# Small bf16 products ahead of unmasked scores, and products of zeros in TensorE's first waits

## The chip, the cores and the metric

The kernel runs on one core of a Trainium2 chip. The metric is the device time of one execution in microseconds, given as the median of several runs. The engines are called PE (TensorE; PEld is its weight load), DVE (VectorE), ACT (ScalarE), POOL (GpSimd) and SP (SyncE, which issues the DMAs).

## The reference

Eight batches of 512 tokens with 256 channels pass through two layers. Each layer is attention, added to its input, and a feed-forward part, added to that. Cut to what matters here (`D` is 16, there are 16 heads):

```
# layer 0, attention on y = layernorm(x): two softmaxes, one causal over the tokens, one over the context
att  = where(causal, (y Wq + bq)(y Wk + bk)^T / sqrt(D), -inf)     # "S": masked scores
attc = (y Wcq + bcq)(ctx Wck + bck)^T / sqrt(D)                    # "C": no mask
x = x + (softmax(att) (y Wv + bv) + softmax(attc) (ctx Wcv + bcv)) Wp + bp
x = x + bitlinear(gelu(bitlinear(layernorm(x))))                   # quantised feed-forward
# layer 1
x = x + (softmax((y Wq + bq)(ctx Wk + bk)^T / sqrt(D)) (ctx Wv + bv)) Wo + bo   # "X": no mask, y = layernorm(x)
x = x + qlinear(gelu(qlinear(layernorm(x))))                       # quantised over the whole tensor
```

## The kernel before

**Units.** The attention work is cut into 24 units: `S`, `C` and `X` for each batch (`UNITS`). A unit has four groups of four heads, 96 groups in all (`G`). Two groups share a "stack": queries and keys are split into a high and a low part and laid by DMA into 48 rows of `qk_t` for each half of the partitions (rows 0 and 64), so that one product gives the scores of one head with more precision than one part holds. `stack_job` issues six DMAs of 256 KB for it.

**Three kinds of steps** pass over each group:

- `max_one` computes scores with queries on the partitions into a pair of PSUM banks (two heads at once, one in each half of the rows), and DVE reduces each row to its maximum. For `C` and `X` a step is one tile of 128 queries by 512 keys; for `S` the causal mask comes first.
- `rows_job` turns the maxima and lays them into rows 48 and 49 of the stack, so that the next scores come out with the maximum taken off.
- `exp_one` computes the scores again, keys on the partitions, 50 rows deep, into two banks, and ACT takes the exponential of each.
- `av_part` multiplies the exponentials with the values, four heads side by side in tiles of 128 rows by 32 columns.

For `S` units `masks` puts the mask into the bank before the scores: for each half of the rows two small bf16 products of an identity and a mask (64 rows), and the scores accumulate onto them. `C` and `X` units have no such products; there the first score product begins the bank.

**Tile shapes.** The projections, the values and the output products go through `wide`, four column tiles of 128x32 side by side ("cols"). Scores and masks use two row tiles of 64x128 ("rows"). Other products use the whole array ("full"). A "visit" in this text is a stretch of row-tiled steps between two stretches of the other kinds.

**The order** is not written by hand. The class `Plan` holds a clock for each engine and costs for each step, and a loop at the end of `build` takes, at each moment, the step or job that is due: maxima, exponentials, values, or one of the jobs (projections, feed-forward, evacuations), which are generators that yield the time when they want to go on. `plan.pe(cols, mode)` adds a step's cost and notes the tile shape in `plan.mode`; a change of shape costs `SWITCH`. The order that comes out is fixed at build time, and each engine works through its own list. `Writer.matmul` adds, for the first product into a bank under a new name, waits for all who read the bank before.

**The start.** `first_x` and the first two weights are loaded by DMA, then eight small DMAs of biases and eight of identity and mask are issued by SP. `ln_job` for the first tokens takes statistics in `stats` (four `bn_stats`, four `bn_aggr`), DVE normalises, PE turns the tokens (32 products, two records each in the profile), and `prep_job` for the first two stacks projects queries and keys; DVE and ACT split them, `stack_job` stacks them by DMA, and only then can the first scores run.

Of the kernel before, what the change touches and what calls it, by code (L numbers as in the profile page):

```python
# [9 lines left out]
BF16 = mybir.dt.bfloat16  # L10
SYNC = mybir.DependencyInfo(mybir.DependencyClass.Sync, mybir.DependencyReason.DATA)
# [5 lines left out]
NB, T, C, CC, H, D, FF = 8, 512, 256, 128, 16, 16, 1024  # L17
P = 128
# [206 lines left out]
GQ, AHEAD = 4, 3  # L225
LINGER = 0.2
ROW_COLS = 600
DVE_HANDICAP = 0.8


# [56 lines left out]
def build(tc, A, out):  # L287
    nc = Engines(tc)
# [8 lines left out]
    plan = Plan()  # L297
# [6 lines left out]
    pairs, banks = nc.pairs, nc.banks  # L304
# [44 lines left out]
    zero = const.tile([P, 1], F32, name="zero")  # L349
    nc.vector.memset(zero, 0.0)  # L350
    one = const.tile([P, 1], F32, name="one")
    nc.vector.memset(one, 1.0)
    ones_sq = one.broadcast_to([P, P])

    ident2 = const.tile([P, 2, P], BF16, name="ident2")
    mask2 = const.tile([P, 2, P], BF16, name="mask2")
# [105 lines left out]
    def used(key, tag, t):  # L462

        uses[key][0] -= 1
        uses[key][1] = max(uses[key][1], t)
        if not uses[key][0]:
            give(tag, uses[key][1])

    def stats(x, nm):

        st = wp.tile([P, NT, 6], F32, tag="bnst", name=f"st_{nm}", bufs=3)
        mv = wp.tile([P, NT, 2], F32, tag="bnmv", name=f"mv_{nm}", bufs=3)
        r = wp.tile([P, NT], F32, tag="rstd", name=f"r_{nm}", bufs=3)
        neg = wp.tile([P, NT], F32, tag="nmean", name=f"nm_{nm}", bufs=3)
        for t in range(NT):
            nc.vector.bn_stats(st[:, t, :], x[:, t, :])
            op("dve", C)
            yield plan.now + 0.4
        for t in range(NT):
            nc.vector.bn_aggr(mv[:, t, :], st[:, t, :])  # L480
        te = plan.run("dve", 0.4)
        nc.gpsimd.tensor_scalar(r, mv[:, :, 1], LN_EPS, 0.0, ALU.add, ALU.add)
        nc.gpsimd.tensor_tensor(r, r, mhalf, ALU.pow)
        nc.gpsimd.tensor_scalar(neg, mv[:, :, 0], -1.0, 0.0, ALU.mult, ALU.add)
        te = plan.run("pool", 1.3, te)
        return mv[:, :, 1], neg, r, te
# [63 lines left out]
    def prep_job(n):  # L550
        kind, b = UNITS[n // 2]
        u = n % 2
        yield from take("qkt")
        tt = tile("qkt", [P, 4, T], F32R, f"qkt{n}")
        tl = []

        def split(wname, ps, pb, tm, hi, lo):

            full = tt[:, lo, :].bitcast(F32)
            nc.scalar.activation(full, ps, AF.Identity, bias=qk_bias[:, BIDX[wname], u : u + 1])  # L560
            t = op("act", T + 110, tm)
            give_bank(pb, t)
            yield t + LAT
            if n < 2:
                nc.vector.tensor_copy(tt[:, hi, :], full)
                th = op("dve2", T, t)
                nc.vector.tensor_tensor(tt[:, lo, :], full, tt[:, hi, :].bitcast(F32), ALU.subtract)
                tl.append(op("dve", T))
            else:
                copy_ts(tt[:, hi, :], full)  # L570
                th = op("pool", T, t)
                low_part(tt[:, lo, :], full, tt[:, hi, :])
                tl.append(op("pool2", T, th))
            return th

        ready = []
        for i, (hi, lo) in enumerate(((0, 1), (3, 2))):
            wname, which = KIND[kind][i]
            key, ring = src_key(kind, b, which)
            yield from until(key, ("w", wname, u))  # L580
            xs = xlt[key]
            nk = xs.shape[1]
            ps, pb = yield from gen_bank()
            for k in range(nk):
                yield pe_next()
                wide(ps, WT[wname][:, u, k], xs[:, k, :], k == 0, k == nk - 1)
                tm = plan.pe(4 * T, "cols")
            used(key, ring, tm)
            ready.append((wname, ps, pb, tm, hi, lo))
            if n >= 2 or i == 1:  # L590
                for r in ready:
                    th = yield from split(*r)
                ready = []
        qkt_t[n] = (tt.bitcast(F32), tl)
        at["qkt", n] = max(tl[0], th)
# [50 lines left out]
    def masks(ps, c, blocks, keys):  # L646
# [5 lines left out]
        for k in range(2):  # L652
# [5 lines left out]
                start=k == 0, stop=False, skip_group_check=True,  # L658
            )

    def max_ready(s):
        G, i = MAX_STEPS[s]
        t = plan.bank_at("sm")
        if ("stack", G) not in at or t is None or (i == 0 and G % 2 == 0 and not plan.rings["mx"]):
            return None
        return max(at["stack", G], t)

    def max_one(s):

        G, i = MAX_STEPS[s]  # L670
        kind, _ = UNITS[G // 4]
        p, qts = MAXS[kind][i]
        n = G // 2
        if i == 0 and G % 2 == 0:
            heapq.heappop(plan.rings["mx"])
            mx_t[n] = tile("mx", [P, 2, 4, NT], F32, f"mx{n}")
        pb = plan.bank_take("sm")
        ps = pairs[pb // 2]
        pair = 2 * (G % 2) + p
        size = [(qt + 1) * P if kind == "S" else T for qt in qts]  # L680
        offs = [sum(size[:x]) for x in range(len(qts))]
        if kind == "S":

            first = size[0] // P - 1
            step = size[-1] // P
            for c in range(2):
                masks(ps[:, c], c, slice(first, first + (len(qts) - 1) * step + 1, step), False)
            plan.pe(len(qts) * 192 + 60, mode="rows")
        for off, w, qt in zip(offs, size, qts):
            for c in range(2):  # L690
                q, k = (qk_t[n % NQK][64 * c : 64 * c + 48, pair, x] for x in range(2))
                nc.tensor.matmul(
                    ps[:, c, off : off + w], q[:, qt * P : (qt + 1) * P], k[:, :w],
                    start=off == 0 and kind != "S", stop=True, skip_group_check=True,
                )
        t = plan.pe(sum(size), mode="rows")
        for off, w, qt in zip(offs, size, qts):
            nc.vector.tensor_reduce(
                mx_t[n][:, :, pair, qt], ps[:, :, off : off + w], AX.X, ALU.max, negate=True
            )  # L700
            t = op("dve", 2 * w, t)
        plan.bank_give("sm", pb, t)
        if s + 1 == len(MAX_STEPS) or MAX_STEPS[s + 1][0] != G:
            at["max", G] = t
# [51 lines left out]
    def exp_one(s):  # L756


        G, i = EXP_STEPS[s]
        kind, _ = UNITS[G // 4]  # L760
        p, kts = EXPS[kind][i]
        n = G // 2
        pair = 2 * (G % 2) + p
        pb = plan.bank_take("st", 2)
        tp, slots = zip(*(heapq.heappop(plan.p_free) for _ in range(2)))
        pt = [wp.tile([P, T], F32, tag=f"p{slots[c]}", name=f"p{G}_{i}_{c}", bufs=1) for c in range(2)]
        ps, off = [banks[x] for x in pb], 0
        if kind == "S":
            step = (T - kts[0] * P) // P
            for c in range(2):  # L770
                masks(ps[c], c, slice(0, (len(kts) - 1) * step + 1, step), True)
            plan.pe(len(kts) * P + 80, mode="rows")
        for kt in kts:
            q0 = kt * P if kind == "S" else 0
            w = T - q0
            for c in range(2):
                q, k = (qk_t[n % NQK][64 * c : 64 * c + 50, pair, x] for x in range(2))
                nc.tensor.matmul(
                    ps[c][:, off : off + w], k[:, kt * P : (kt + 1) * P], q[:, q0:],
                    start=off == 0 and kind != "S", stop=True, skip_group_check=True,  # L780
                )
                p_t[G, kt, 2 * p + c] = pt[c][:, off : off + w]
            off += w
        t = plan.pe(off, mode="rows")
        if s + 1 == len(EXP_STEPS) or EXP_STEPS[s + 1][0] != G:
            at["exp", G] = t
        tm = t
        for c in range(2):
            nc.scalar.activation(pt[c][:, :off], ps[c][:, :off], AF.Exp, scale=0.25)
            t = op("act", off, tm, tp[c])  # L790
            plan.bank_give("st", pb[c], t, c == 1)
        for kt in kts:
            p_at[G, kt, p] = t
        p_slots[G, kts[-1], p] = slots
# [799 lines left out]
    for bs in ((0,), (1,), (2, 3), (4, 5), (6, 7)):  # L1594
        n, b = len(bs), bs[0]
        if b == 4:
            split_b2()
        for f in range(8):
            i = 8 * b + n * f
            ps = [banks[2 + i % 6]] if n == 1 else [pairs[1 + f % 3][:, x] for x in range(2)]  # L1600
# [86 lines left out]
    for i in range(2 * NB):  # L1687
# [4 lines left out]
        ps = half_ps.pop(i, None)  # L1692
        if ps is None:
            ps = bias_first(i)
# [79 lines left out]
```

## Time and profile before

| | us |
|---|---|
| median of 3 runs | 1464.75 |
| lowest and highest | 1461.56 to 1465.69 |
| the profiled execution's own time | 1460.25 |
| its span, first to last instruction | 1458.4 |
| mean granted TensorE clock over the span | 0.971 |

| engine | busy us | share | instructions |
|---|---|---|---|
| PE | 1374.8 | 94% | 14400 |
| PEld | 597.5 | 41% | 14400 |
| DVE | 1142.0 | 78% | 1591 |
| ACT | 1035.5 | 71% | 1904 |
| POOL | 681.6 | 47% | 1025 |

All engines work at once, so the shares are not to be added. Products on PE overlap in the records: a product's record runs from its start to its end, and the next one may start before that end, so the distance from one start to the next tells more than the length of a record. A float32 product has two records, a product of the stacks (marked f32 in the profile) or of bf16 has one. `48*128` in a row of the profile means 48 rows and 128 columns of the array. The granted clock is the share of TensorE's full clock that the chip let through in a window of time.

### The profile page before, as it was taken

The numbers are of one execution on the slowest core, as the hardware profiler recorded it, in microseconds if no ns is written. First come the engines' busy times: TensorE is split into PE (matmuls) and PEld (weight loads), VectorE is DVE, ScalarE is ACT, GpSimd is POOL, SyncE is SP. The second block draws the span as 40 slices with busy tenths as digits, with TensorE's granted clock in tenths as the row PEclk, the third lists the DMA queues.
The fourth block names the chain that finished last, engine by engine and source line by source line (L and its number), as shares of the span: only waits on it lengthen the run. The fifth ranks groups of instructions, "written<-read, shape, count | busy, mean of one in ns | idle before, by whom it ended". The sixth has DMA issues, their size and how long they took to land. (4 is left out here: it accounts for less than half of the span.)

```text
span 1458.4 us, 36089 instructions
## 1 busy us (share of the span) xinstructions
PE 1374.8 (94%) x14400; PEld 597.5 (41%) x14400; DVE 1142.0 (78%) x1591; ACT 1035.5 (71%) x1904; POOL 681.6 (47%) x1025
## 2 busy tenths in 40 slices
PE   4999999999999999999999999999999998999978
PEld 2443444444444444434344433443333333333527
DVE  4678588697788886898777996689899888766397
ACT  1456767677768867767677777668778795777587
POOL 1463355465455465464653552654455541524332
PEclk8899999999999999999899999999999999999899
DMA  6593565667576755665457655556647657373343
GB/s 126 152 216 76 133 139 125 142 138 182 132 161 150 161 129 141 156 161 126 105 126 155 163 126 132 142 120 160 163 105 169 155 149 196 105 176 110 117 142 116
DMA packets 155612, 207.03 MB, mean 142 GB/s; under 512 B 71940, under 2 KB 74244, under 8 KB 154932
## 3 DMA queue, kind: packets, MB, share of 16 engines
q1 hardware_dynamic: 155444, 204.73, 58.0%
q8 instruction: 113, 1.85, 0.5%
q14 instruction: 55, 0.45, 0.1%
HBM read 68.15 MB, written 47.43 MB: 79 GB/s over the span
## 5 line engine op out<-in xcount | busy, mean ns | idle before, releaser
L241 DVE TENSOR_REDUCE mx<-pair 128x2 f32<-128x1024 f32 (+3 forms) x768 | 808.9, 1086 | 210.7 <-PE pair L259 194.6
L241 ACT ACTIVATE p<-bank 128x512 f32<-128x512 f32 (+1 forms) x1408 | 712.0, 587 | 232.7 <-PE bank L259 224.8
L259 PE MATMUL bank<-p,v 128*32 128x512 f32 (+3 forms) x3072 | 371.7, 563 | 2.9 <-DVE mrow L241 1.3
L259 PE MATMUL bank<-qk 50*128 50x512 f32 (+3 forms) x1536 | 337.6, 433 | 16.2 <-ACT p L241 8.0
L259 PE MATMUL pair<-qk 48*128 48x512 f32 (+3 forms) x1536 | 325.5, 438 | 25.7 <-DVE mx L241 11.8
L259 PEld LDWEIGHTS bank<-qk 50*128 50x128 f32 x1536 | 159.6, 190 | 215.7 <-ACT p L241 142.9
L259 PEld LDWEIGHTS pair<-qk 48*128 48x128 f32 x1536 | 148.0, 191 | 171.5 <-DVE mx L241 83.4
L384 POOL TENSOR_SCALAR qkt<-qkt 128x512 fp32r<-128x512 f32 x92 | 57.1, 621 | 164.1 <-ACT qkt L241 157.5
L241 ACT ACTIVATE qkt<-bank,qk_bias 128x512 f32<-128x512 f32 x96 | 66.6, 693 | 81.0 <-PE bank L259 65.4
L409 POOL TENSOR_TENSOR qkt<-qkt 128x512 fp32r<-128x512 f32 x92 | 118.8, 1291 | 7.7
L259 PEld LDWEIGHTS bank<-p,v 128*32 128x32 f32 x3072 | 70.9, 109 | 114.6 <-issue 85.9
L384 POOL TENSOR_SCALAR mhl<-mx 128x32 fp32r<-128x32 f32 x48 | 11.8, 245 | 171.3 <-DVE mx L241 164.8
L883 POOL TENSOR_TENSOR yt<-oc,rb 128x512 f32<-128x512 f32 x31 | 39.8, 1283 | 73.3 <-DMA rb<-scrz 50.9
L259 PE MATMUL pair<-mask,ident 64*128 64x128 bf16 (+2 forms) x768 | 58.0, 226 | 6.9 <-DVE mx L241 4.7
L259 PE MATMUL bank<-ident,mask 64*128 64x64 bf16 (+1 forms) x768 | 52.7, 206 | 3.7 <-ACT p L241 1.2
L259 PEld LDWEIGHTS <-ident 64*128 64x128 bf16 x768 | 26.1, 97 | 71.0 <-issue 52.8
L259 PEld LDWEIGHTS <-mask 64*128 64x128 bf16 x768 | 25.8, 96 | 69.3 <-issue 61.0
L241 ACT COPY v<-bank 128x512 f32<-128x512 f32 x44 | 26.2, 596 | 39.4 <-PE bank L259 39.1
L241 ACT COPY ev<-bank 128x512 f32<-128x512 f32 x56 | 33.5, 598 | 17.9 <-PE bank L259 17.9
L241 DVE SCALAR_TENSOR_TENSOR h<-bank,so,bc_l_b 128x512 f32<-128x512 f32 x64 | 45.3, 741 | 0.9 <-PE bank L259 0.7
L241 ACT ACT_TABLE_LOAD x34 | 43.6, 1283 | 1.9 <-PEq L1762 0.7
L1189 POOL TENSOR_SCALAR h<-h,sh 128x1024 f32<-128x1024 f32 x32 | 36.0, 1125 | 17.7 <-DVE sh L241 15.2
(230 smaller groups left out, 1686.4 us busy)
## 6 DMA issues: line engine op xcount, KB each, us to landing
qk<-qkt SPq DMA_DIRECT2D x288, 256.0 KB
scro<-ev SPq DMA_DIRECT2D x94, 256.0 KB
oc<-scro SPq DMA_DIRECT2D x47, 256.0 KB
rb<-scrz SPq DMA_DIRECT2D x47, 256.0 KB
x_d<-xb SPq DMA_DIRECT2D x15, 512.0 KB
xa_s<-in_x SPq DMA_DIRECT2D x8, 512.0 KB
xb<-in_x SPq DMA_DIRECT2D x8, 512.0 KB
xr<-x_d SPq DMA_DIRECT2D x16, 256.0 KB
```

The lines of the kernel that those rows point to most:

```text
L241: r = f(*args, **kw)
L259: r = self.eng.matmul(out, *args, **kw)
L384: nc.gpsimd.tensor_scalar(dst, src, 1.0, 0.0, ALU.mult, ALU.add)
L409: nc.gpsimd.tensor_tensor(dst, full, high.bitcast(F32), ALU.subtract)
L883: nc.gpsimd.tensor_tensor(y, o, rb, ALU.mult)
L1189: nc.gpsimd.tensor_scalar(ht, ht, s[:, t - t0 : t - t0 + 1], MAGIC, ALU.mult, ALU.add)
```

## The change

Two things are added; nothing is taken away, and `Plan` is not told of either, so its order of steps stays as it is.

1. `first_of_visit` is called at the head of every unmasked step of `max_one` and `exp_one` when `plan.mode` is not `rows`, that is when the step follows column-tiled or whole-array products. It issues, for each half of the rows, one bf16 product of 64 rows by 128 columns over 16 moving columns (`NFIRST`), of the identity and the mask, into the first 16 columns of the bank that the scores are about to begin. The scores start the bank anew, so nothing of it stays.
2. `keep_warm` issues products of zeros: a zero column spread to 128x128 as weights, and spread to 512 moving columns, into bank 6 (through `pairs[3]`). There are eight right after the constants are set, two behind each of the four `bn_stats` of the first tokens and three more behind the last of them, and 24 after the last projection of the second stack.

```
+NFIRST = 16
...
+    zero_b = zero.bitcast(BF16)[:, 0:1]
+
+    def keep_warm(n, behind=None):
+
+        for _ in range(n):
+            r = nc.tensor.matmul(
+                pairs[3][:, 0], zero_b.broadcast_to([P, P]), zero_b.broadcast_to([P, T]), start=True, stop=True
+            )
+            if behind is not None:
+                tc.add_manual_dep(r.ins, behind.ins.name, SYNC, reason="warm")
+                behind = None
+
+    keep_warm(8)
...
-            nc.vector.bn_stats(st[:, t, :], x[:, t, :])
+            r_st = nc.vector.bn_stats(st[:, t, :], x[:, t, :])
+            if nm == "s0":
+                keep_warm(2, r_st)
...
         te = plan.run("dve", 0.4)
+        if nm == "s0":
+            keep_warm(3, r_st)
...
             used(key, ring, tm)
+            if (n, i) == (1, 1):
+                keep_warm(24)
...
+    def first_of_visit(ps):
+
+
+        if plan.mode != "rows":
+            for c in range(2):
+                rows = slice(64 * c, 64 * c + 64)
+                nc.tensor.matmul(
+                    ps[c][:, :NFIRST], ident2[rows, 0], mask2[rows, 0, :NFIRST], start=True, stop=True,
+                    skip_group_check=True,
+                )
...
             plan.pe(len(qts) * 192 + 60, mode="rows")
+        else:
+            first_of_visit([ps[:, c] for c in range(2)])
...
             plan.pe(len(kts) * P + 80, mode="rows")
+        else:
+            first_of_visit(ps)
```

## The prediction

> **What bounds the kernel now.** I read the page's engine shares first, then busy time by stage, then TensorE's waits, then the order of time around single visits to the scores, then the start.
>
> ```profile
> PE 1374.8 (94%) x14400; PEld 597.5 (41%) x14400; DVE 1142.0 (78%) x1591; ACT 1035.5 (71%) x1904; POOL 681.6 (47%) x1025
> PEclk8899999999999999999899999999999999999899
> ```
>
> TensorE (PE) leads; its granted clock is low only in the first slices. By stage (us, then busy time and count of PE, its weight loads PEld, DVE, ACT, POOL; then clock, DMA share, GB/s):
>
> ```profile
> 400.00:800.00 400.00, 386.70 (x4494) 168.59 (x4487) 323.63 (x469) 290.38 (x542) 206.41 (x304) 0.97 0.63 143
> 800.00:1200.00 400.00, 385.19 (x3970) 154.56 (x3966) 338.56 (x456) 306.56 (x579) 201.76 (x308) 0.99 0.60 143
> ```
>
> From 64 to 1365 us, where the attention steps run, PE is idle for 46 of 1301 us, in 94 gaps over 0.1 us; VectorE and ScalarE have a fifth free. TensorE's largest waits there (us in total, times, longest):
>
> ```profile
> PE pair L259 <- DVE mx L241: 13.4, 25, 1.6
> PE bank L259 <- ACT p L241: 9.8, 18, 2.2
> ```
>
> So time added to TensorE in the middle mostly reaches the end, and a gain there mostly too, until one of these two becomes late. Now one unmasked visit, column-tiled products (128*32), then three score steps of 512 columns (start, duration):
>
> ```profile
> 661.34 1.06 PE L259 MATMUL bank<-p,v 128*32 128x512 f32 x8
> 662.34 0.50 PE L259 MATMUL pair<-qk 48*128 48x512 f32 x2
> 662.68 0.40 PE L259 MATMUL bank<-qk 50*128 50x512 f32 x2
> 662.91 0.40 PE L259 MATMUL pair<-qk 48*128 48x512 f32 x2
> ```
>
> The first step holds TensorE from 662.34 to 662.68, the second only to 662.91. The medians over the trace are 338 ns for a first step and 237 for a following one: a visit pays 101 ns at its door. That is the weight load: it starts 2 ns before the first product[...]. A visit that has masks ahead, products first and then the loads:
>
> ```profile
> 805.14 0.23 PE L259 MATMUL bank<-ident,mask 64*128 64x64 bf16 x4
> 805.21 0.48 PE L259 MATMUL bank<-qk 50*128 50x512 f32 x2
> 805.53 0.41 PE L259 MATMUL pair<-qk 48*128 48x512 f32 x2
> ```
> ```profile
> 805.14 0.12 PEld L259 LDWEIGHTS <-mask 64*128 64x128 bf16 x4 [0.41 <-issue]
> 805.18 0.20 PEld L259 LDWEIGHTS bank<-qk 50*128 50x128 f32 x2
> ```
>
> Here the score load starts at 805.18, when the second mask product of its half starts, and the next step stands at 805.53.
>
> **Part 1, the small products.** The order of instructions has 11519 products in the changed program against 10664: 855 more, of which 8 + 4×2 + 3 + 24 = 43 are zeros, so 812 are the 16-column ones, two to a visit: 406 visits, 184 for maxima and 222 for exponentials. All 406 lie between 60 and 1360 us, in the TensorE-bound stretch. Nothing else moves: the other engines keep their order.
>
> The trace has no 16-column product, but the masks are the same form with 64 to 256 columns. Set at the first mask load's start, the medians of 28 visits are: second mask load at 15 ns, second mask product at 43, score load at 45, next score step at 391. With 128 mask columns the score load is at 72 and the next step at 418. So the next step comes 346 ns after the score load starts, whatever stood ahead; and a load can start 15 ns after the one before it[...]. With one small product per half the score load moves to 15 (instead of 0), the next step to 15 + 346 = 361, against 338 + 2 = 340 to 342 today: 19 to 21 ns more. [...] I take **19 ns**. Bounds: 49 from above (387 − 338, all four mask products); from below −82, if the product hid the load wholly (237 + 19 − 338).
>
> [...] The row: in all 406 unmasked first steps, 16 of which wait for no semaphore, the load starts 1 or 2 ns before the product, never earlier; and behind masks it starts 2 ns after the last mask product begins. [...] by the row it is 406 × 19 ns = 7.7 us. I take the row.
>
> How much of 7.7 reaches the end? I laid 19 ns on each of the 406 places of the trace and carried it along each engine's order and each semaphore, with the slack that each wait showed. 5.9 us come out (75%): the rest is caught in gaps where DVE or ACT was late for a reason of its own. At 10 ns it is 3.0 us, at 25 ns 7.9, at 49 ns 16. **+5.9 us.**
>
> **Part 2, waits that move.** A score product no longer waits for its bank; the small one does. Queued behind it are the scores, which waited before: no loss. But 110 ScalarE exponentials get a second wait, on ScalarE's own semaphore, long fulfilled. In the trace an exponential with PE's wait alone starts 22 ns after that semaphore rises (165 of them), with both 82 ns (31); when ScalarE is behind, the overlap with the one before shrinks from 126 to 104 ns. 62 of the 110 were waiting and 48 behind: 62 × 60 + 48 × 22 = 4.8 us of ScalarE, which feeds the column products; carried on as above it adds **1.2 us** (0 to 1.6). Three table loads now carry a wait: each was followed at once by work, so PE was ready, 0 us; if not, at most 1.28 us each on ScalarE.
>
> **Part 3, the start.** 19 products of zeros run from 1.6 us until about 8, before the first real product:
>
> ```profile
> 9.16 3.59 PE L259 MATMUL bank<-ident_r,xa_s 128*32 128x128 f32 x64 [9.16 <-DVE xa_s L241]
> 12.57 1.95 PE L259 MATMUL bank<-xlt_s,w_Sq 128*32 128x512 f32 x16
> ```
>
> 64 products in 16 rounds of 2×128 columns should take 1.7 us at full rate (projection rounds of 2×512 take 0.43); they take 3.4[...]. Warm, this saves 1.7 us of TensorE. But VectorE first copies the second weights (14.74 to 15.62, their DMA lands at 14.7), and only then casts the projections; the stacks' DMAs wait for that. Carried on, 1.7 becomes **−0.3 us**. The clock's windows are 3.41 us long and this execution's began just at 9.15[...]. In the timed runs I add −0.8, the middle.
>
> The 24 zeros take about 24 × 0.22 = 5.2 us (512 columns at full rate), from 19.1 to 24.3, while the first stack lands at 27: they are hidden. ([...] the clock stood at 1.00 there.)
>
> ```profile
> 22.81:26.22 3.41, 0.00 (x0) 0.00 (x0) 0.00 (x0) 0.00 (x0) 0.00 (x0) 0.50 1.07 180
> 26.22:29.63 3.41, 1.31 (x8) 1.12 (x9) 0.00 (x0) 0.00 (x0) 0.00 (x0) 0.50 1.07 189
> 29.63:33.05 3.42, 2.55 (x27) 2.07 (x22) 3.14 (x6) 0.00 (x0) 0.00 (x0) 0.50 1.07 188
> 33.05:36.46 3.41, 3.01 (x25) 1.97 (x22) 3.19 (x4) 0.00 (x0) 0.00 (x0) 0.50 1.07 197
> ```
>
> [...] windows with PE busy for 2.55 to 3.16 of 3.41 us stayed at 0.50, and VectorE is busy for 3.1 to 3.2 of 3.4 there, so a faster PE would wait for it. If the whole stretch were warm, carrying it on gives −1.2 us; if only up to 29.6, −0.4. I take **−0.4**.
>
> **Sum.** +5.9 + 1.2 − 0.3 − 0.4 = +6.4 us on the profiled execution (span 1458.4, its own time 1460.25): 1466.7. The median of the three runs, 1464.75, lies 4.5 above that one; on it, with the −0.8 for the phase, +5.6: **1470.3 us**.
>
> **Rivals.**
> A, the forecast: the load is put off by 15 to 25 ns. 1467 to 1474 by the sizes above. 0.66, of which 0.17 within 0.3% (that is ±4.4 us, about what a measurement of this kernel can tell from no change).
> B, nothing measurable: the delays fall into the 46 us of PE's gaps and the start pays for the rest; +1 to +3, about 1467. For it: 94 gaps among 406 visits. Against: they are clustered. 0.14.
> C, faster: [...] It decides from the point where a visit's door falls under 338 ns in all; at −20 ns a visit the carrying gives −4 to −5 us, at −82 it gives −15 to −17, about 1449. Against it speak the constant 346 ns and the masked visits, which show the same form without any such gain. 0.13.
> D, slower by more: each small pair costs what four mask products do, 49 ns, 16 us: about 1481. 0.07.
>
> C and D lie outside the range of 1462 to 1476: two in ten. Slower: 0.49 + 0.07; same: 0.17 + 0.14; faster: 0.13.
>
> **What would show it.** In the changed profile a visit's score load should start 15 ns after the small load and the next step 357 to 362 ns after the door; PE's busy time should grow by some 5 us of zeros and 8 of visits. The transposes should take 1.7 us, yet the first scores start no earlier than about 26.6 us, and the clock should be at 0.50 by 30 us. The forecast is wrong if the door-to-next-step time is at or under 338 ns, if it is near 390, or if VectorE's reduction of the first scores starts over 1.5 us earlier.

## The result and the profile after

| | before | after |
|---|---|---|
| median, run side by side | 1462.47 us (16 runs) | 1472.62 us (16 runs) |
| lowest and highest | 1457.72 to 1468.91 | 1464.48 to 1480.73 |
| profiled execution's own time | 1460.25 | 1464.48 |
| its span | 1458.4 | 1462.7 |

The ratio of the times is 1.0066, with a 95% interval of 1.0047 to 1.0085: the change costs 9.6 us (6.9 to 12.4). The profiled execution is the fastest of its 16 and has the highest granted clock of them (0.979, where their mean is 0.970), so its span shows less of the loss than the median does.

The page of the changed kernel, engine shares and granted clock:

```profile
PE 1384.0 (95%) x15248; PEld 607.5 (42%) x15255; DVE 1142.1 (78%) x1591; ACT 1035.4 (71%) x1904; POOL 679.5 (46%) x1025
...
PEclk8999999999999999999999999999999999999999
```

TensorE has 9.2 us more work and is still the busiest engine (95%). By stage (us, then busy time and count of PE, PEld, DVE, ACT, POOL; clock, DMA share, GB/s):

```profile
400.00:800.00 400.00, 384.17 (x4682) 169.55 (x4678) 321.86 (x467) 289.15 (x540) 205.76 (x303) 0.99 0.64 143
800.00:1200.00 400.00, 384.79 (x4255) 157.37 (x4258) 335.52 (x454) 303.44 (x572) 199.27 (x306) 0.99 0.60 142
```

The counts of PE grew by 188 and 285, its busy time did not, because a product's record covers part of the next one (0.07 us of it at 664.35 below) and, in the first row, because the clock was higher (0.99 against 0.97); VectorE, ScalarE and GpSimd get through 1 to 7 instructions fewer per 400 us. The price therefore has to be read from distances between starts. The same visit as before the change, column-tiled products first:

```profile
663.35 1.07 PE L260 MATMUL bank<-p,v 128*32 128x512 f32 x8
...
664.35 0.10 PEld L260 LDWEIGHTS <-ident 64*128 64x128 bf16 x2 [0.84 <-issue]
664.35 0.18 PE L260 MATMUL bank<-mask,ident 64*128 64x16 bf16 x2
664.35 0.20 PEld L260 LDWEIGHTS bank<-qk 50*128 50x128 f32 x2
664.39 0.48 PE L260 MATMUL bank<-qk 50*128 50x512 f32 x2
...
664.71 0.40 PE L260 MATMUL pair<-qk 48*128 48x512 f32 x2
```

From the first small product (664.35) to the next step (664.71) it is 0.36 us, where the first score step held TensorE for 338 ns before. The score load does not start ahead of the small load (both at 664.35; 7 ns behind it in the medians of the first round's visits alone), and the column-tiled products' record ends (664.42; the ends of products are modelled in the profile) after both have started; it did so before the change too (662.40, with the score load at 662.34). TensorE's waits from 64 to 1365 us (total, times, longest):

```profile
PE pair L260 <- DVE mx L242: 12.3, 26, 1.6
PE bank L260 <- ACT p L242: 10.8, 22, 2.2
PE bank L260 <- DMA qk<-mrow: 5.8, 4, 2.6
PE pair L260 <- DMA qk<-qkt: 3.5, 7, 0.9
```

The two waits that lead are as they were (13.4 and 9.8 before). The two below them are waits for a DMA to land, and they grew; the rows of before are shown under the second round of experiments. Last, the start, TensorE's rows and then four windows of the clock:

```profile
1.66 5.97 PE L260 MATMUL pair<-zero 128*128 128x512 bf16 x19 [1.66 <-DVE one L242]
9.14 2.27 PE L260 MATMUL bank<-ident_r,xa_s 128*32 128x128 f32 x64 [1.51 <-DVE xa_s L242]
11.23 1.94 PE L260 MATMUL bank<-xlt_s,w_Sq 128*32 128x512 f32 x16
...
15.89 1.93 PE L260 MATMUL bank<-xlt_s,w_Sq 128*32 128x512 f32 x16 [1.00 <-DVE w_Sq L242]
...
19.69 5.20 PE L260 MATMUL pair<-zero 128*128 128x512 bf16 x23 [0.16 <-issue]
24.82 0.34 PE L260 MATMUL pair<-mask,ident 64*128 64x256 bf16 x4
27.87 0.33 PE L260 MATMUL pair<-qk 48*128 48x128 f32 x1 [2.70 <-DMA qk<-qkt]
```
```profile
24.83:28.24 3.41, 0.66 (x6) 0.29 (x5) 0.00 (x0) 0.00 (x0) 0.00 (x0) 1.00 1.07 177
28.24:31.65 3.41, 1.92 (x14) 1.65 (x16) 1.41 (x3) 0.00 (x0) 0.00 (x0) 0.50 1.07 193
31.65:35.07 3.42, 2.94 (x24) 2.10 (x24) 3.09 (x5) 0.00 (x0) 0.00 (x0) 0.50 1.07 189
35.07:38.48 3.41, 2.75 (x24) 2.09 (x22) 3.30 (x6) 0.00 (x0) 0.00 (x0) 0.50 1.06 276
```

The transposes take 2.1 us instead of 3.4. Then the projections stand still until 15.89 for the second weights, and the first scores start at 27.87, 0.6 us later than before the change. The first stack's DMA sets that moment. The clock is at half from 28.24 to 41.90 (before the change from 22.81 to 43.29).

### The profile page after: what moved, and what is told of

Same layout as the page of the kernel before. It is cut to its first block, busy times and chain, and to the rows that moved or that the text cites. A ratio compares the mean times of both kernels' runs of the same rounds, so it can differ in the third digit from the quotient of the medians.

```text
span 1462.7 us, 37895 instructions
## 1 busy us (share of the span) xinstructions
PE 1384.0 (95%) x15248; PEld 607.5 (42%) x15255; DVE 1142.1 (78%) x1591; ACT 1035.4 (71%) x1904; POOL 679.5 (46%) x1025
## 4 chain that ended last, share of the span: by engine, by line
PE 69%; DVE 9%; DMA 8%; ACT 7%; POOL 3%; issue 3%; SPq 2%; ACTq 0%; POOLq 0%; DVEq 0%
PE bank L260 55%; PE pair L260 14%; DVE mx L242 5%; DMA qk<-qkt 4%; ACT p L242 3%; DVE gmax L242 2%; DMA qk<-mrow 1%; ACT L242 1%; ACT jq L242 1%; SPq L627 1%; ACT h L242 1%; DMA hqt<-hq 1%; DMA y<-y_d 1%; DMA tyt<-tyq 0%; DVE am L242 0%
## 5 line engine op out<-in xcount | busy, mean ns | idle before, releaser
L260 PE MATMUL bank<-p,v 128*32 128x512 f32 (+3 forms) x3072 | 366.4, 556 | 2.9 <-DVE mrow L242 1.3
L260 PE MATMUL bank<-qk 50*128 50x512 f32 (+3 forms) x1536 | 331.8, 425 | 17.3 <-ACT p L242 8.1
L260 PE MATMUL pair<-qk 48*128 48x512 f32 (+3 forms) x1536 | 319.7, 430 | 19.4 <-DVE mx L242 8.9
L260 PEld LDWEIGHTS <-ident 64*128 64x128 bf16 x1580 | 65.9, 94 | 354.7 <-issue 311.3
L260 PE MATMUL pair<-mask,ident 64*128 64x128 bf16 (+3 forms) x1136 | 91.7, 211 | 8.9 <-DVE mx L242 6.6
```

The source lines that it names most:

```text
L260: r = self.eng.matmul(out, *args, **kw)
```

## First round: the two halves of the change, and the visits by kind

All edits are against the changed kernel, except for one control in the second round; each kernel was run beside the kernel before, 6 to 22 times. To say where a loss lies I laid the TensorE steps of each trace beside those of before, from 64 to 1360 us, and added up the differences of the distances from one step's start to the next, in three groups: at the doors (the step that opens a visit and the one after it, together), at steps that follow an idle time of TensorE of over 30 ns in either trace ("waits"), and at steps in half-clock windows of either trace. What is left is under 2 us. A step can follow an idle time inside a half-clock window; counting it in one group or the other moves these two sums against each other by up to some 2.5 us, so only their larger differences say something.

**Visits alone.**

```
-        for _ in range(n):
+        for _ in range(0):        # keep_warm: no zeros
```

> The small products alone, no zeros. Theory (the door of a visit is 19 ns longer, and nearly all of it reaches the end): the whole loss of the change, +7 to +10 us on before, and the door-to-next-step time at 356 ns against 338. Rival 'the start costs' (the zeros delay the second weights' DMA or the first stack): +4 to +6 only, and the rest appears in the run of the zeros alone.

Measured: 1476.16 us, ratio 1.0096 (1.0070 to 1.0122), +14 us. Doors +7.6 us, which is 406 × 19 ns almost to the digit; waits +2.2, half-clock places +5.8. So the price at the door was sized rightly, and there is a second loss away from the doors.

**Zeros alone.**

```
-        if plan.mode != "rows":
+        if False:                 # first_of_visit: no small products
```

> The 43 products of zeros alone, no small products. Theory: -2 to 0 us (the transposes take 2.1 instead of 3.4 us, but the first stack's DMAs wait for the second weights; clock back at 0.50 by 30 us). Rival 'the start costs': +2 to +4 us, with the second weights' DMA landing 0.7 us later as in the changed kernel. Rival 'the warm clock carries on': -5 us or more.

Measured: 1469.14 us, ratio 1.0049 (1.0028 to 1.0070), +7 us. 43 products of zeros, all done by 25.0 us, cost as much as the 812 small products at their doors. Nothing changed at any door; waits +3.5, half-clock places +1.9. No part of the forecast held such a term.

**Small products for the maxima only** (184 visits; ScalarE's exponentials keep their single wait) and **for the exponentials only** (222 visits, with all the second waits on ScalarE); both without zeros.

```
@@ exp_one (maxima only)
-        else:
-            first_of_visit(ps)
@@ max_one (exponentials only)
-        else:
-            first_of_visit([ps[:, c] for c in range(2)])
```

> The small products only at the 184 visits that begin with maxima; no zeros; no ScalarE wait changes. Theory: 184/406 of the visits' loss, 184 x 19 ns = 3.5 us if all of it reaches the end, 2.6 at 75%. Rival 'ScalarE's second waits make the loss': 2 us or less here and nearly all in the exponentials.

> The small products only at the 222 visits that begin with exponentials; no zeros; ScalarE's 110 second waits are all there. Theory: 222 x 19 ns = 4.2 us plus 1 us from the waits, 4 to 5.5 us. Rival 'ScalarE's second waits make the loss': 7 us or more.

Measured: 1.0067 (1.0041 to 1.0093) and 1.0064 (1.0041 to 1.0087). The doors give 3.3 us (18 ns each) and 4.4 us (20 ns each); what remains is 6.5 us without the second waits on ScalarE and 4.9 with them. The 1.2 us that I had set down for these waits do not show, though the intervals (±3.5 us) cannot exclude so small a sum. By these medians the remainder is again about as large as for zeros alone; each stands on only six runs.

## Second round: a loss that does not ask what is added

**The kernel before against itself** (a comment is the only edit).

> The kernel before itself, as a control of what the comparison can tell. Theory: ratio 1.000 within 0.2%, so the +0.5% of the zeros alone is real. Rival 'scatter': a ratio of 1.002 to 1.005 here, and the zeros' loss is within what two sets of runs of one program differ by.

Measured: 0.9994 (0.9974 to 1.0014). The method finds no difference where there is none, so the zeros' +7 us is more than the scatter between two sets of runs.

**The same 43 zeros with 16 columns**, **only the 19 before the first tokens**, and **only the 24 behind the second stack's projections**; no visits in any of them.

```
e6 -  pairs[3][:, 0], zero_b.broadcast_to([P, P]), zero_b.broadcast_to([P, T]), ...
   +  pairs[3][:, 0, :16], zero_b.broadcast_to([P, P]), zero_b.broadcast_to([P, 16]), ...
e7 -  if (n, i) == (1, 1):
   -      keep_warm(24)
   +      pass
e8 -  keep_warm(8)
   ...
   -      keep_warm(2, r_st)
   +      pass
   ...
   -      keep_warm(3, r_st)
   +      pass
```

> All 43 products of zeros with 16 moving columns instead of 512, no small products at visits: the same instructions, hardly any TensorE activity. Theory 'activity at the start changes which later windows are cold': 0 us on before. Rival 'more instructions in TensorE's list': +4 to +6 us as with the full zeros. Rival 'scatter': within 2 us of the control.

> Only the 19 products of zeros before the first tokens. By the chain of the start: -1 to +0.5 us (transposes 2.1 us instead of 3.4 to 3.6, the second weights' DMA 0.7 us later if it is these zeros that hold it up). If these 19 carry the zeros' loss: +4 to +6 us.

> Only the 24 products of zeros after the second stack's projections. By the chain of the start: -0.5 to +0.5 us, since they end before the first stack lands and the clock still falls to 0.50 by 30 us. If these 24 carry the zeros' loss: +4 to +6 us, and the other run near 0.

Measured: 1.0048 (1.0031 to 1.0064), 1.0044 (1.0028 to 1.0060) and 1.0058 (1.0036 to 1.0080). The work of the zeros is not the cause, since a thirty-second of the columns costs the same within the intervals; nor is it a sum over them, since 19 or 24 cost about what 43 do, nor the place in the start. And the start's own timing is not: VectorE's first reduction begins at 30.2 us in the first two and at 29.4 in the third, 0.3 us earlier than in the kernel before. The traces put the loss at waits: +6.2, +6.8 and +6.8 us. Here are TensorE's waits for DMAs from 64 to 1365 us (total, times, longest), the kernel before first, then the 16-column zeros, then the 24 zeros:

```profile
PE bank L259 <- DMA qk<-mrow: 4.6, 2, 2.7
PE pair L259 <- DMA qk<-qkt: 2.2, 6, 0.6
```
```profile
PE pair L260 <- DMA qk<-qkt: 6.3, 9, 2.2
PE bank L260 <- DMA qk<-mrow: 5.4, 3, 2.7
...
PE bank L260 <- DMA hqt<-hq: 1.6, 3, 1.0
```
```profile
PE bank L260 <- DMA qk<-mrow: 7.3, 4, 2.9
PE pair L260 <- DMA qk<-qkt: 4.6, 8, 1.3
...
PE bank L260 <- DMA hqt<-hq: 1.5, 1, 1.5
```

6.8 us became 13.3 and 13.4: TensorE stands longer for stacks (`qk`) and the transposed `hqt`, though no edit touches a DMA. It is a matter of single transfers: from issue to landing those of the stacks (`qk<-qkt`) take 5.99 us in the mean before, and 6.05 and 5.99 in these two. The page tells what else uses the DMAs. Its line for queue q8 (packets, MB, share of 16 engines) is of the programs' own instruction lists, first in the kernel before, then in the changed one, then in the one with the 24 zeros:

```profile
q8 instruction: 113, 1.85, 0.5%
```
```profile
q8 instruction: 120, 1.97, 0.6%
```
```profile
q8 instruction: 113, 1.85, 0.6%
```

So the amount fetched is not what costs: the kernel with the 24 zeros fetches as much as the one before. The lists are fetched in packets of 16 KB, and one takes 1.1 us in the records, where a data packet of 2 KB takes 0.14, about the same for each byte. The theory for the last round, which no trace had shown, was that a transfer that TensorE is about to need lands late if such a packet stands in its way, and that instructions put early into TensorE's list move all later packet boundaries.

## Third round: does the place of the instructions matter?

**The small products twice**, four to a visit, no zeros.

```
-            for c in range(2):
+            for c in (0, 1, 0, 1):
```

> No zeros; the two small products of each of the 406 visits are issued twice (four to a visit). So far the visits alone gave 13.4 us over the kernel before, of which the trace shows 7.6 us at the doors; zeros of any kind gave about 6.5 us with nothing at the doors. Theory 1, a fixed loss of some 6 us as soon as TensorE's program is longer, plus a price per door: the second pair moves the score load by one more load (15 to 20 ns a visit, 6 to 8 us), so about +20 us, ratio 1.014 (1.0125 to 1.0155), and the door at about 373 to 380 ns. Theory 2, all that the visits cost is in proportion to their number of products, nothing is fixed: twice 13.4, +27 us, ratio 1.018. Theory 3, the second pair passes wholly under the first one's loads: as with one pair, 1.0096.

Measured: 1481.59 us, ratio 1.0135 (1.0104 to 1.0165), +20 us, as the first theory (a constant plus a price per door) said; twice the loss of single visits (1.019) lies outside, if not by much. The doors give 15.8 us, 7.6 for the first pair and 8.2 for the second (20 ns each). A visit of this kernel:

```profile
672.84 0.21 PE L260 MATMUL pair<-mask,ident 64*128 64x16 bf16 x4
672.91 0.48 PE L260 MATMUL pair<-qk 48*128 48x512 f32 x2
673.22 0.39 PE L260 MATMUL bank<-qk 50*128 50x512 f32 x2
```

From the first small product to the next step it is 0.38 us, against 0.36 with one pair: each pair moves the next step by another 20 ns. The score load itself moves otherwise: in the medians it starts 7 ns after the first small load with one pair and 45 ns after it with two, and the next step follows it by 353 and then by 340 ns.

**One product of zeros at the start**; **24 zeros of 16 columns behind the program's last product**; **23 more tiny instructions on VectorE at the start** (24 in place of one; the expectation counts one too many). No visits and no other zeros in any of them.

```
e10 -        for _ in range(n):
    +        for _ in range(1 if n == 8 else 0):
e11 +    for _ in range(24):
    +        nc.tensor.matmul(ps[:, 0, :16], zero_b.broadcast_to([P, P]), zero_b.broadcast_to([P, 16]), start=True, stop=True)
         ctx.close()
e12 +    for _ in range(24):
             nc.vector.memset(one, 1.0)
```

> No visits and a single product of zeros at the start (one weight load and one product more on TensorE). Theory 1, any lengthening of TensorE's program costs the fixed loss, through where its instructions come to lie: +6 us, 1.004 to 1.005. Theory 2, the loss comes of some tens of instructions (fetching them), or of their work: two instructions cost nothing, 1.000 within 0.0015.

> No visits and no zeros at the start; 24 zeros of 16 columns stand behind the last product of the program instead, where TensorE has no more work. They move no instruction in time until 1455 us. Theory 1, a shift in time early on sets off other landings of DMAs later: nothing lost here, 1.000, at most 1 us more at the end. Theory 2, the place or the length of the program in memory makes the loss, whatever the products do: 1.004 to 1.005.

> No visits and no zeros; VectorE sets the same small constant 25 times instead of once, in its first microseconds, before the first tokens land. Theory 1, what counts is that TensorE's instruction list grows: nothing lost, 1.000 within 0.0015. Theory 2, any change of the program (its length, or where its instructions lie) costs the fixed loss: 1.004 to 1.005.

Measured: 0.9994 (0.9975 to 1.0013), 0.9990 (0.9971 to 1.0010) and 1.0006 (0.9993 to 1.0019). None of the three costs anything. So it is not the length of TensorE's program (the second adds as many zeros as the kernel with 24 did), nor that there is an edit, nor an early shift in time: the first two had their first reduction 0.8 and 1.0 us later than before, more than any kernel with the constant loss and without visits. What costs in these runs is some tens of instructions (19 are enough, at 1.0044) on TensorE ahead of its work or among it.

All kernels side by side. The packet column adds up the waits of TensorE for DMAs (those of at least 150 ns, 64 to 1365 us) during whose last 3.5 us a 16 KB list packet was on its way. The column "equal clock" is worked out from the timed runs, each of which has its mean granted clock on record: over all of them 0.001 of clock goes with 0.95 us, and the column gives the loss in us that is left when kernels are compared at one clock (standard error 0.5 to 1.0; the runs of before beside the changed kernel have no clock on record):

| kernel | ratio | equal clock | doors | waits | half clock | waits for DMAs | of these with a list packet |
|---|---|---|---|---|---|---|---|
| before (profile) | | | 0 | 0 | 0 | 6.8 | 0.3 |
| before again | 0.9994 | −0.4 | 0 | +0.9 | −2.0 | 7.5 | 1.3 |
| one zero | 0.9994 | +0.6 | 0 | +1.4 | +1.5 | 8.4 | 1.0 |
| zeros at the end | 0.9990 | −0.9 | 0 | +0.6 | +6.1 | 9.1 | 1.4 |
| 23 more on VectorE | 1.0006 | +0.3 | 0 | +0.7 | +4.4 | 8.5 | 0.6 |
| zeros of 16 columns | 1.0048 | +4.6 | 0 | +6.2 | +2.2 | 13.3 | 6.6 |
| 19 zeros | 1.0044 | +4.6 | 0 | +6.8 | +1.8 | 10.5 | 5.6 |
| 24 zeros | 1.0058 | +9.0 | 0 | +6.8 | +2.1 | 13.4 | 6.1 |
| all 43 zeros | 1.0049 | +5.5 | 0 | +3.5 | +1.9 | 11.9 | 5.6 |
| maxima only | 1.0067 | +5.3 | +3.3 | +3.4 | +4.2 | 12.0 | 4.2 |
| exponentials only | 1.0064 | +6.8 | +4.4 | +1.9 | +3.1 | 9.7 | 4.0 |
| visits | 1.0096 | +12.0 | +7.6 | +2.2 | +5.8 | 10.1 | 3.3 |
| visits twice | 1.0135 | +17.0 | +15.8 | +3.8 | +2.3 | 12.6 | 6.7 |
| changed kernel | 1.0066 | – | +7.2 | +1.4 | −2.6 | 10.2 | 3.5 |

The last column parts the kernels as the ratios do: 0.3 to 1.4 us in the five whose time is that of before, 3.3 to 6.7 in all others. The half-clock column, of the one profiled execution, does not: it is largest in one of the kernels that lose nothing.

Two things weaken this. First, a packet starts about every 12 us, so many waits have one near them by chance. With the packets of each trace shifted along the span at random, the last column comes to 2.9 to 3.5 us in the five and to 4.0 to 5.5 in the others. The kernels that lose hit as chance would have it; it is the five that lie below chance. So the kernel before may owe its time in part to a lucky place of its packets, which an edit early in TensorE's list gives up, rather than the edit having a price of its own. Second, the clock takes a part of the loss. In the timed runs it was 0.9690 in the mean for the kernel before in the second round and 0.9662 and 0.9669 with the 16-column and the 19 zeros, which accounts for 2 to 3 of their 7 us. At equal clock, maxima and exponentials alone add up to the visits (5.3 + 6.8 against 12.0), and beyond the doors the kernels with visits lose 1 to 4 us, those with zeros 5 to 9. A loss of one size in all of them is not what these runs show. Whether a lower clock follows from longer waits or fell to these runs by chance is open.

One transfer shows it closely. It is the last of the six DMAs of a stack that TensorE waits for near 940 us. First the kernel before, then the one with zeros at the end, then the one with 24 zeros at the start (start, duration, and in brackets the idle time and what ended it):

```profile
939.84 0.50 PE L259 MATMUL pair<-qk 48*128 48x512 f32 x1 [0.43 <-DMA qk<-qkt]
```
```profile
948.36 0.49 PE L260 MATMUL pair<-qk 48*128 48x512 f32 x1 [0.98 <-DMA qk<-qkt]
```
```profile
947.12 0.49 PE L260 MATMUL pair<-qk 48*128 48x512 f32 x1 [1.30 <-DMA qk<-qkt]
```

By the trace's DMA records no list packet falls between the issue of this transfer and its landing in the first two, and the product starts 7.3 and 7.9 us after the issue. In the third a packet of 1.0 us starts at 945.18, and it is 8.5 us. Over all traces: 6.7 to 8.0 us in the seven without a packet on its way, 8.4 to 9.4 us in the six with one that begins in the middle or end of the transfer (in the remaining kernel a packet begins just after the issue: 7.9 and 8.5 us for two parts of the stack). Of 245 transfers to the stacks that some traces show with a packet on its way and others without, 216 take longer with one, by 0.5 us in the mean.

No run moved the packets and nothing else, for instance by the same instructions at another place in the list, so that they cause the late landings is a reading of the traces, not shown by an experiment. What is shown is that, of the kernels run, those lose that have tens of instructions ahead of or among TensorE's work, and that their waits for DMAs are longer: 9.7 to 13.4 us, against 6.8 to 9.1 in the five. The waits with a packet on the way make up 3 to 7 us of them, not all of which need be the packet's.

## Why the prediction was right or wrong

The forecast was 1470.3 us, 5.6 over the median it was laid on; measured were 1472.62, and 9.6 over the kernel before. The direction, the size at the door and the range were right. The price of the whole was 4 us too low: a loss away from the doors stood in the sum at nothing, and a gain at the start (−1.5 us) did not come.

- **The door: 19 ns × 406 = 7.7 us. The size was right, its working only in part.** It is 7.6 us in the kernel with visits alone, and 20 ns more a visit for the second pair. In the medians of that kernel the score load starts 7 ns after the small load rather than 15, and the next step 353 ns after that rather than 346; the two errors cancel, and the door stands at 360, inside the 357 to 362 forecast. That they cancel is luck: the time from load to next step is not the same whatever stands ahead (340 ns without small products and with two pairs, 346 behind masks), and of rival A's 15 to 25 ns only 7 are a later load. In the rows the record of the column-tiled products ends after the score load has started, before the change by 0.06 us (662.40 against 662.34). Rivals C (under 338) and D (390) are excluded by the door. In the kernel with visits alone all 406 score loads start 3 ns or more behind the small load, none ahead of it.
- **The share that arrives: 75%, +5.9 us. Open.** The sum of TensorE's waits from 64 to 1365 us, without those for DMAs, was 35.1 us before and 34.4 with visits alone, as if the gaps had caught 0.7 us of 7.6. But in the four kernels with neither visits nor a loss the same sum lies between 35.1 and 36.7, and with visits twice it is 32.6, so 0.7 to 2.3 of 7.6 and 2.5 to 4.1 of 15.8 us are as likely. The second pair adds 8.2 us at the doors and 5.7 to the time (1.0135 less 1.0096, with an uncertainty of about 6). Neither 75% nor the whole is excluded. Rival B (+1 to +3 us) is, by the time itself.
- **ScalarE's second waits: +1.2 us. Misread, and too small to show in the time.** In the trace of before, an exponential that ScalarE stood idle for starts 22 ns after TensorE's semaphore rises with one wait, as forecast, but 48 ns after it with both (54 of them), not 82; in the changed kernel it is 23 and 49 (110 of them). With 26 ns in place of 60 the 4.8 us of ScalarE become 2.7.
- **The start: −0.3 and −0.4 us, and −0.8 for the phase in the timed runs. The order of events was right, the gain is not to be seen.** The transposes took 2.1 us (3.4 before, 1.7 forecast), the second weights came next as the forecast said, but their own DMA, which took 1.43 us to issue (0.53 before), landed later: VectorE copies them at 15.43 instead of 14.74. First scores came at 27.87, with 26.6 as the earliest forecast. The 24 zeros were hidden (done by 24.89). The clock fell at 28.24, after a window in which TensorE was busy for 0.66 of 3.41 us and idle for 2.70 at a stretch, and windows with 2.94 and 2.75 of 3.41 us busy stayed at half, as those with 2.55 to 3.16 had before. The −0.8 was half of an estimated 1.7 us, and no trace here shows that saving. With 43 zeros alone the kernel is 7 us slower, not 1.5 faster.
- **Missing: a loss away from the doors, put at nothing.** By the ratios it is 6 to 8.5 us in the four variants with zeros alone and 4 to 6.5 us beyond the doors in those with visits alone (at equal clock 5 to 9 and 1 to 4), and nothing with one instruction more, with 24 behind the end or with 23 on VectorE. I took added instructions for their time on their engine; the fetching of the program itself, which the page lists as a queue, was not in the sum. Whether that is the cause is not shown.

That the measured time fell into the range of 1462 to 1476 us is in part luck. The visits alone, at 1476.16, stand just outside, and visits (+14) and zeros (+7) do not add up: together they cost 9.6. Had they added up, it would have been some 1484 us. The absolute number was also laid on the median of three runs, 2.3 us above that of the sixteen beside the changed kernel, which brought it nearer. Why the changed kernel lies below the one with visits alone is open. Its profiled execution has less half-clock time behind 50 us (48.6 us; 71.7 with visits alone; 64.9 before), but that is the execution with the highest clock of its 16; over the timed runs the mean clocks, 0.970 and 0.968, would make 1 to 2 us of it. The list packets may fall better in this program, or it may be chance: its interval (1.0047 to 1.0085) and that of the visits alone (1.0070 to 1.0122) overlap.

None of the versions is faster than the kernel before, so there is no better one to propose.

## What to carry to other kernels

In this kernel a small product of another kind ahead of a large weight load did not hide the load; it put the next step off by 20 ns each time. How much of such a delay the gaps catch could not be told here, with TensorE busy 94% of the time: the second pair of products added 8.2 us at the doors and 5.7 (give or take 6) to the time. So carry both cases through a forecast. Before a loss of half a per cent is put down to the instruction that was added, run the same number of instructions with next to no work, and run them behind everything else: here that told the price of the work from the price of the place. Compare such small losses at equal granted clock where the runs have it on record. And lay the instruction queue's packets beside the transfers that the bounding engine waits for, but set what you find against what chance would give.

## What the runs showed that I had not expected

- 43 products with 16 columns, done by 21 us, cost a kernel of 1460 us 0.5%; 24 of the same behind its end made −0.1% (−0.3 to +0.1), which is no difference.
- A 16 KB packet of the instruction list takes 1.1 us in the DMA records, about eight times a 2 KB packet of data, for eight times the bytes. The stack's transfer near 940 us lands after 6.7 to 8.0 us without one and 8.4 to 9.4 with one.
- In the profiled executions of the kernel before and the changed one the stretches of one granted clock last whole multiples of 3.41 us (the first at half lasts six before the change, four after it), but at another phase: it begins at 22.81 and at 28.24 us, 1.6 such steps apart. Single times follow the granted clock: over the runs of the changed kernel 0.001 of clock goes with 0.9 us.
